# Transposing attention by DMA, as two planes of half words, in place of TensorE

## The chip, the cores, the metric

One core of a Trainium2 chip. The metric is the device time of the whole program in microseconds (us).

## The reference

Two graph layers over 128 batches of 128 tokens with 512 features. Layer 0 is attention with 8 heads of 64, whose scores are multiplied by twice the adjacency matrix before the softmax; layer 1 is a graph attention that the change does not touch.

```python
q, k, v = (proj(Wq, bq), proj(Wk, bk), proj(Wv, bv))
scores = jnp.einsum('bhqd,bhkd->bhqk', q, k) * SCALE
mask = (adj_matrix + bond_matrix)[:, None, :, :]
attn = jax.nn.softmax(scores * mask, axis=-1)
ctx = jnp.einsum('bhqk,bhkd->bhqd', attn, v)          # needs attn with k on the partitions
```

The scores come out with q on the partitions, and the context product wants k there, so each head's 128x128 block of attention, in fp32, has to be transposed.

## The kernel before

It works on pairs of batches, a and b, in one turn of a loop of 67. Products of the next group ("units", one call of `unit()`), the output product of the turn before (`output0`) and layer 1 of the turn before that (`output1`) are woven between the pieces of attention, so that TensorE has always something to do. Each engine runs its instructions in the order in which they are written here.

```python
def attn_T(b):
    at = ats[b][0]
    pa = ps2.tile([P, H, S], F32, name="pa", tag="ps2")
    for j in range(H):
        nc.tensor.transpose(pa[:, j, :], at[:, j, :], ident)   # TensorE, 8 heads
    aT = work.tile([P, H, S], F32, name="aT")
    nc.scalar.copy(aT, pa)                                     # ScalarE, PSUM to SBUF
...
# one turn, cut to a's and b's attention; o and e are the turns of output0 and output1
    scores(a); unit()()
    ...exps, normalise(a)...
    gather1(e, 0); gather1(e, 1); unit
    attn_T(a)
    output1(e, 0); output1(e, 1); unit
    context(a); unit()()
    scores(b)
    ...exps, normalise(b)...
    attn_T(b); hidden1(o); unit()(); output1(e, 5); output1(e, 6)
    context(b)
```

`context` ends with a ScalarE copy of its result to `cxT`; `unit()()` is a product and its eviction, in even turns often a ScalarE copy to v.

Of the kernel before, what the change touches and what calls it, by code (L numbers as in the profile page):

```python
# [7 lines left out]

F32 = mybir.dt.float32
AF = mybir.ActivationFunctionType  # L10
OP = mybir.AluOpType
AX = mybir.AxisListType

P = 128
# [3 lines left out]
H = 8  # L18
# [5 lines left out]
def kernel(  # L24
# [70 lines left out]
    def load_adjT(p):  # L95
        adjTs[p] = aio.tile([P, 2, S], F32, name="adjT")
        nc.sync.dma_start(adjTs[p], both(adjT, p))
# [71 lines left out]

        return mv, stats, power  # L170

    st0, rows0, qks, vs, ats, l1s, zs = {}, {}, {}, {}, {}, {}, {}

    def stats0(p, src):
        st0[p], stats, power = row_stats(src)
# [25 lines left out]

    def fetch0(p):
        r = rows0[p]
        rows0[p] = small.tile([P, 2, 2 * S], F32, name="mr", bufs=2)
        nc.sync.dma_start(
            rows0[p].rearrange("p s k -> p (s k)"), r.rearrange("s b p -> (s b p)").partition_broadcast(P)
        )
# [98 lines left out]
    def scores(b):  # L306
        p, i = divmod(b, 2)
        g, h = divmod(p, 2)
        qT, kT = qks[g, "q"][h], qks[g, "k"][h]
        cols = slice(i * S, (i + 1) * S)  # L310

        sc = ps2.tile([P, H, S], F32, name="sc", tag="ps2")
        for j in range(C):
            for s in range(2):
                r = slice(s * D, (s + 1) * D)
                nc.tensor.matmul(sc[:, s * C + j, :], qT[r, j, cols], kT[r, j, cols], start=True, stop=True)  # L316
        at = work.tile([P, H, S], F32, name="at")
        nc.vector.scalar_tensor_tensor(  # L318
            at, sc, QSCALE, adjs[p][:, i : i + 1, :].to_broadcast([P, H, S]), op0=OP.mult, op1=OP.mult
        )  # L320
        nmx = small.tile([P, H], F32, name="nmx")
        nc.vector.tensor_reduce(nmx, at, AX.X, OP.max, negate=True)  # L322
        ats[b] = at, nmx, small.tile([P, H], F32, name="sums")

    def exps(b, heads):
        at, nmx, sums = ats[b]
        for j in heads:
            nc.scalar.activation(at[:, j, :], at[:, j, :], AF.Exp, bias=nmx[:, j : j + 1], accum_out=sums[:, j : j + 1])  # L328

    def normalise(b):  # L330
        at, _, sums = ats[b]
        rs = small.tile([P, H], F32, name="rs")
        nc.vector.reciprocal(rs, sums)
        nc.vector.tensor_tensor(at, at, rs[:, :, None].to_broadcast([P, H, S]), OP.mult)  # L334

    def attn_T(b):
        at = ats[b][0]
        pa = ps2.tile([P, H, S], F32, name="pa", tag="ps2")
        for j in range(H):
            nc.tensor.transpose(pa[:, j, :], at[:, j, :], ident)  # L340
        aT = work.tile([P, H, S], F32, name="aT")
        nc.scalar.copy(aT, pa)  # L342
        ats[b] = aT


    cxT = const.tile([P, 7, 2, S], F32, name="cxT")
# [5 lines left out]
    def context(b):  # L352

        p, i = divmod(b, 2)
        aT = ats.pop(b)
        pc = ps1.tile([P, C, S], F32, name="pc", tag="ps1")
        for j in range(C):
            for s in range(2):
                head = 2 * j + s
                nc.tensor.matmul(  # L360
                    pc[s * D : (s + 1) * D, j, :], vs[b // G][:, b % G, head * D : (head + 1) * D], aT[:, s * C + j, :],
                    start=True, stop=True,
                )
        nc.scalar.copy(rows_of(cxT, i), pc)  # L364
# [74 lines left out]
    def scale1(p):  # L439
        h2, w, sums = l1s[p]  # L440
        rs = small.tile([P, 2], F32, name="rs1")
        nc.vector.reciprocal(rs, sums)
        nc.vector.tensor_tensor(w, w, rs[:, :, None].to_broadcast([P, 2, S]), OP.mult)  # L443
        l1s[p] = h2, w, work.tile([P, 7, 2, S], F32, name="gT")
# [97 lines left out]
    with tc.manual_schedule():  # L542
# [28 lines left out]
        for p in range(N + 3):  # L571
            g, odd = divmod(p, 2)
            units = (SEQ[10:] if odd else SEQ[:10]) if (g + 1) * 2 < N else []
            units = iter(units)

            def unit():
                u = next(units, None)
                return product(g + 1, u[0], int(u[1])) if u else lambda: None

            attn = p < N  # L580
            o = p - 1 if 0 <= p - 1 < N else None
            e = p - 2 if 0 <= p - 2 < N else None
            f = p - 3 if 0 <= p - 3 < N else None
            h = p + 4 if p + 4 < N else None
            a, b = 2 * p, 2 * p + 1


            if o is not None:
                load_adjT(o)
            if p + 1 < N:  # L590
                load_adj(p + 1)
            if h is not None:
                fetch0(h)
                load_xT(h)
            if p + 5 < N:
                load_x0(p + 5)
            if attn:
                scores(a)
            unit()()

            if e is not None:
                scores1(e)
            if attn:
                exps(a, range(4))
            if o is not None:

                first, second = output0(o, 0), output0(o, 1)
                first()
                second()
            if e is not None:  # L610
                softmax1(e)
            if p == 1:
                spread_u()
            done = unit()
            if e is not None:
                scale1(e)
            done()
            if attn:
                exps(a, range(4, H))

            if o is not None:
                output0(o, 2)()
            done = unit()
            if attn:
                normalise(a)
            done()
            if f is not None:
                finish_a(f)

            if e is not None:  # L630
                gather1(e, 0)
                gather1(e, 1)
            done = unit()
            if f is not None:
                finish_b(f)
            done()
            if e is not None:
                gather_sums(e)

            if attn:  # L640
                attn_T(a)
            if e is not None:
                first, second = output1(e, 0), output1(e, 1)
                first()
                second()
            if o is not None:
                context_sums(1)
            if attn and p > 2:
                load_x(p)
            done = unit()  # L650
            done()
            if h is not None:
                hidden(h)

            if attn:
                context(a)
            unit()()
            if p + 5 < N:
                stats0(p + 5, x0s.pop(p + 5))

            if attn:
                scores(b)
            if o is not None:
                output0(o, 3)()
            if p == 0:
                constant_c()
                weight_sums(wo_sb)
            unit()()
            if attn:
                exps(b, range(4))  # L670

            if o is not None:
                output0(o, 4)()
            if e is not None:
                output1(e, 2)()
            if attn:
                exps(b, range(4, H))
            unit()()
            if odd and (g + 2) * 2 < N:
                hidden_sums(g + 2)  # L680
            if p + 5 < N:
                spread0(p + 5)

            if o is not None:
                output0(o, 5)()
                stats1(o, 0)
            if attn:
                normalise(b)
            if e is not None:
                output1(e, 3)()  # L690
            unit()()

            if o is not None:
                output0(o, 6)()
                stats1(o, 1)
            if e is not None:
                output1(e, 4)()
            done = unit()
            if attn:
                shift(p)  # L700
            done()

            if attn:
                attn_T(b)
            if o is not None:
                hidden1(o)
            unit()()
            if e is not None:
                output1(e, 5)()
            if o is not None:  # L710
                dots1(o, 0)
            if e is not None:
                output1(e, 6)()
            if attn:
                context(b)
            if o is not None:
                dots1(o, 1)
            if e is not None:
                elu(e)
            if attn:  # L720
                context_sums(0)
            if p == 0:
                constant_u()
                weight_sums(w1_sb)
# [42 lines left out]
```

## Time and profile before

| | before |
|---|---|
| median of 4 runs | 2589.59 us (2589.25 to 2589.99) |
| TensorE, VectorE, ScalarE busy | 98%, 79%, 50% |
| mean granted clock of TensorE | 0.993 |
| one pair of turns, even and odd | 78.3 us |

Busy is the share of the span in which an engine worked; the granted clock is the share of full speed that TensorE was given. In the profiles below PE is TensorE, PEld its loading of weights, DVE VectorE, ACT ScalarE, POOL GpSimd and SPq the queue that issues DMAs; the chain is the work that ended last, followed back from the last instruction through what each step waited for. pa are the transposes, sc the scores, pc the contexts, acc the units' products, row the output products of both layers, gT the evicted gathers; sp and tp are the planes before and after the DMA; x16 counts instructions. The pair of turns was read as the time from one scores product to the fourth after it, which is the same for nearly all pairs. The lines are shown in the prediction.

### The profile page before, as it was taken

How to read it: one execution, taken by the hardware profiler on the slowest of the kernel's cores; microseconds unless marked ns; L12 is line 12 of the kernel's file. 1: busy time of each engine (PE TensorE's matmuls, PEld its weight loads, DVE VectorE, ACT ScalarE, POOL GpSimd, SP SyncE). 2: the span in 40 equal slices, each digit the busy share in tenths (PEclk: the TensorE clock that was granted, in tenths of full speed). 3: DMA queues.
4: the chain of work that ended last, by engine and by line, in shares of the span. 5: the costliest groups of instructions: out<-in, count | busy, mean ns of one | idle time of the engine just before them, and what ended most of it. 6: DMA issues, size and time to landing. Idle time of an engine off the chain costs nothing.

```text
span 2589.1 us, 40551 instructions
## 1 busy us (share of the span) xinstructions
PE 2531.6 (98%) x15288; PEld 2162.4 (84%) x15288; DVE 2050.1 (79%) x3781; ACT 1300.3 (50%) x3915; POOL 119.7 (5%) x263
## 2 busy tenths in 40 slices
PE   8899999999999999999999999999999999999986
PEld 7788888888888888888888888888888888888875
DVE  5677888878888878888878888878888878887775
ACT  3345455455554554554554554454554555555553
POOL 0000000000000000000000000000000000000000
PEclk9899999999999999999999999999999999999998
DMA  3122222222222222222222222222222222221001
GB/s 138 50 62 66 63 77 66 61 78 66 61 75 69 61 71 74 61 70 69 66 63 79 62 65 66 74 66 62 78 66 62 78 66 61 78 66 54 30 31 43
DMA packets 192868, 171.84 MB, mean 66 GB/s; under 512 B 41376, under 2 KB 135584, under 8 KB 192032
## 3 DMA queue, kind: packets, MB, share of 16 engines
q1 hardware_dynamic: 191088, 169.24, 22.8%
q8 instruction: 120, 1.97, 0.4%
q14 instruction: 76, 0.62, 0.2%
q10 hardware_dynamic: 1584, 0.01, 0.0%
HBM read 135.53 MB, written 33.68 MB: 65 GB/s over the span
## 4 chain that ended last, share of the span: by engine, by line
PE 80%; DVE 9%; ACT 7%; issue 3%; DMA 1%; POOL 0%; SPq 0%; POOLq 0%; DVEq 0%; ACTq 0%
PE acc_a L249 21%; PE row_a L301 16%; PE acc_c L249 11%; PE row_c L301 8%; PE acc_b L249 6%; PE pg L451 5%; PE pa L340 4%; PE sc L316 4%; DVE junk L413 4%; PE pc L360 4%; ACT at L328 2%; DVE at L318 2%; ACT aT L342 1%; ACT w L436 1%; ACT qT L266 1%
## 5 line engine op out<-in xcount | busy, mean ns | idle before, releaser
L328 ACT ACTIVATE at<-at,nmx 128x128 f32<-128x128 f32 x1024 | 396.4, 389 | 34.3 <-DVE nmx L322 32.0
L301 PE MATMUL row_a<-wo,cxT 128*128 128x256 f32 x1280 | 323.1, 383 | 10.9 <-DVE x L374 10.6
L301 PE MATMUL row_a<-w,gT 128*128 128x256 f32 x1280 | 319.0, 380 | 1.8 <-ACT z L478 0.9
L301 PEld LDWEIGHTS row_a<-wo,cxT 128*128 128x128 f32 x1280 | 236.0, 191 | 48.5 <-DVE x L374 20.4
L301 PEld LDWEIGHTS row_a<-w,gT 128*128 128x128 f32 x1280 | 235.9, 191 | 31.1 <-ACT z L478 1.7
L266 ACT ACTIVATE kT<-acc_a,bk 128x256 f32<-128x256 f32 x256 | 107.1, 470 | 290.9 <-PE acc_a L249 290.9
L328 ACT ACTIVATION_READ_ACCUMULATOR at<-at,nmx 128x1 f32 x1024 | 192.8, 188 | 0.0
L163 DVE BATCH_NORM_STATS2 st<-x 128x6 f32<-128x512 f32 x256 | 175.1, 684 | 8.9 <-DMA x<-in_x 4.5
L261 ACT COPY v<-acc_a 128x512 f32<-128x512 f32 x128 | 75.0, 586 | 185.3 <-PE acc_a L249 185.3
L342 ACT COPY aT<-pa 128x1024 f32<-128x1024 f32 x128 | 129.6, 1012 | 74.9 <-PE pa L340 70.1
L266 ACT ACTIVATE qT<-acc_a,bq 128x256 f32<-128x256 f32 x256 | 106.7, 467 | 110.9 <-PE acc_a L249 110.9
L334 DVE TENSOR_TENSOR at<-at,rs 128x1024 f32<-128x1024 f32 x128 | 156.8, 1225 | 4.4
L322 DVE TENSOR_REDUCE nmx<-at 128x8 f32<-128x1024 f32 x128 | 156.2, 1220 | 4.4
L374 DVE TENSOR_TENSOR x<-row_a,x 128x256 f32<-128x256 f32 x320 | 134.9, 422 | 31.2 <-PE row_a L301 24.7
L318 DVE SCALAR_TENSOR_TENSOR at<-sc,adj 128x1024 f32<-128x1024 f32 x128 | 154.3, 1206 | 4.5 <-PE sc L316 4.5
L316 PEld LDWEIGHTS sc<-kT,qT 64*128 64x128 f32 x2048 | 125.0, 188 | 32.2 <-issue 32.2
L451 PEld LDWEIGHTS pg<-w,h 128*128 128x128 f32 x1024 | 127.7, 200 | 26.7 <-ACT qT L266 15.2
L316 PE MATMUL sc<-kT,qT 64*128 64x128 f32 x2048 | 149.7, 286 | 0.0
L360 PEld LDWEIGHTS pc<-aT,v 128*64 128x64 f32 x2048 | 109.9, 137 | 43.6 <-issue 32.2
L364 ACT COPY cxT<-pc 128x512 f32<-128x512 f32 x128 | 75.0, 586 | 141.5 <-PE pc L360 136.6
L451 PE MATMUL pg<-w,h 128*128 128x128 f32 x1024 | 133.6, 286 | 12.1 <-DVE w L443 5.1
L360 PE MATMUL pc<-aT,v 128*64 128x128 f32 x2048 | 140.9, 280 | 1.1 <-ACT aT L342 1.1
(130 smaller groups left out, 5052.9 us busy)
## 6 DMA issues: line engine op xcount, KB each, us to landing
x<-in_x SPq DMA_DIRECT2D x123, 512.0 KB, 4.6
out<-x SPq DMA_DIRECT2D x64, 512.0 KB, 2.8
hA<-in_xT SPq DMA_DIRECT2D x120, 256.0 KB, 4.2
mr<-rows SPq DMA_DIRECT2D x60, 256.0 KB, 4.2
adj<-in_adj SPq DMA_DIRECT2D x64, 128.0 KB, 10.7
adjT<-in_adjT SPq DMA_DIRECT2D x64, 128.0 KB, 9.0
x<-in_x SPq DMA_DIRECT2D x4, 256.0 KB, 3.9
wv<-in_wvT SPq DMA_DIRECT2D x1, 1024.0 KB
```

The lines of the kernel that those rows point to most:

```text
L163: nc.vector.bn_stats(st, src[:, i, :])
L249: nc.tensor.matmul(acc[:, m, :], lhsT, rhs, start=fresh and m == 0 and c == 0, stop=c == 1, skip_group_check=True)
L266: nc.scalar.activation(dst(t, f)[:, m, :], a[:, m, :], AF.Identity, bias=bias[:, j : j + 1])
L301: nc.tensor.matmul(acc, left[:, la, c, :], w[:, wb, c, :], start=n in (0, 3) and c == 0, stop=c == 1, skip_group_check=True)
L316: nc.tensor.matmul(sc[:, s * C + j, :], qT[r, j, cols], kT[r, j, cols], start=True, stop=True)
L318: nc.vector.scalar_tensor_tensor(at, sc, QSCALE, adjs[p][:, i : i + 1, :].to_broadcast([P, H, S]), op0=OP.mult, op1=OP.mult)
L322: nc.vector.tensor_reduce(nmx, at, AX.X, OP.max, negate=True)
L328: nc.scalar.activation(at[:, j, :], at[:, j, :], AF.Exp, bias=nmx[:, j : j + 1], accum_out=sums[:, j : j + 1])
L334: nc.vector.tensor_tensor(at, at, rs[:, :, None].to_broadcast([P, H, S]), OP.mult)
L342: nc.scalar.copy(aT, pa)
L360: nc.tensor.matmul(pc[s * D : (s + 1) * D, j, :], vs[b // G][:, b % G, head * D : (head + 1) * D], aT[:, s * C + j, :], start=True, stop=True,
L451: nc.tensor.matmul(pg[:, c, :], h2[:, i, c * P : (c + 1) * P], w[:, i, :], start=True, stop=True)
```

## The change

The intent is to take the transposes, 8 matmuls a batch, from TensorE. The DMA engines can transpose elements of two bytes, so ScalarE parts each half of the normalised attention (4 heads) into two planes of half words, one DMA transposes both, and ScalarE joins them to words again. The contexts are moved: a's stands directly before b's scores, b's in the next turn before the next scores.

```diff
-    def attn_T(b):
...
+    def words(a):
+        return a.rearrange("p h k -> p (h k)").bitcast(U16).rearrange("p (k w) -> p w k", w=2)
+
+    def part(b, half):
         at = ats[b][0]
...
+        sp = work.tile([P, 2, C * S], U16, name="sp", bufs=2)
+        nc.scalar.copy(sp, words(at[:, half * C : (half + 1) * C]))
+        tp = work.tile([P, 2 * C, S], U16, name="tp", bufs=2)
+        nc.sync.dma_start_transpose(tp, sp.rearrange("p w k -> p (w k)"))
+        flips[b, half] = tp
+
+    def join(b, half):
...
+        tp = flips.pop((b, half))
+        nc.scalar.copy(words(aTs[b][:, half * C : (half + 1) * C]), tp.rearrange("p (w h) k -> p w (h k)", w=2))
...
+                context(2 * o + 1)          # start of a turn: b of the turn before, then scores(a)
...
-                normalise(a)
+                normalise(a, 1)
             done()
+            if attn:
+                part(a, 1)                  # part(a, 0) a little earlier
...
-                attn_T(a)
...
+            unit()()
+            if attn:
+                join(a, 0)
+                join(a, 1)
...
                 context(a)
+                scores(b)                   # was one unit later
...
                 output1(e, 5)()
+            if attn:
+                join(b, 0)
             if o is not None:
                 dots1(o, 0)
             if e is not None:
                 output1(e, 6)()
-            if attn:
-                context(b)
             if o is not None:
                 dots1(o, 1)
+            if attn:
+                join(b, 1)
```

(The exps are also split otherwise, the first context sums stand later, and some buffers change their number.)

More of the change, by code (lines that the diff above doesn't have):

```diff
@@ L9 @@
 F32 = mybir.dt.float32
+U16 = mybir.dt.uint16
 AF = mybir.ActivationFunctionType
@@ L170, in row_stats @@
         return mv, stats, power
-    st0, rows0, qks, vs, ats, l1s, zs = {}, {}, {}, {}, {}, {}, {}
+    st0, rows0, qks, vs, ats, aTs, flips, l1s, zs = {}, {}, {}, {}, {}, {}, {}, {}, {}
     def stats0(p, src):
@@ L203, in fetch0 @@
         r = rows0[p]
-        rows0[p] = small.tile([P, 2, 2 * S], F32, name="mr", bufs=2)
+        rows0[p] = small.tile([P, 2, 2 * S], F32, name="mr", bufs=1)
         nc.sync.dma_start(
@@ L316, in scores @@
                 nc.tensor.matmul(sc[:, s * C + j, :], qT[r, j, cols], kT[r, j, cols], start=True, stop=True)
-        at = work.tile([P, H, S], F32, name="at")
+        at = work.tile([P, H, S], F32, name="at", bufs=2)
         nc.vector.scalar_tensor_tensor(
@@ L328, in exps, with normalise @@
             nc.scalar.activation(at[:, j, :], at[:, j, :], AF.Exp, bias=nmx[:, j : j + 1], accum_out=sums[:, j : j + 1])
-    def normalise(b):
+    def normalise(b, half):
         at, _, sums = ats[b]
-        rs = small.tile([P, H], F32, name="rs")
-        nc.vector.reciprocal(rs, sums)
-        nc.vector.tensor_tensor(at, at, rs[:, :, None].to_broadcast([P, H, S]), OP.mult)
-    def attn_T(b):
-        at = ats[b][0]
-        pa = ps2.tile([P, H, S], F32, name="pa", tag="ps2")
-        for j in range(H):
-            nc.tensor.transpose(pa[:, j, :], at[:, j, :], ident)
-        aT = work.tile([P, H, S], F32, name="aT")
-        nc.scalar.copy(aT, pa)
-        ats[b] = aT
+        heads = slice(half * C, (half + 1) * C)
+        rs = small.tile([P, C], F32, name="rs")
+        nc.vector.reciprocal(rs, sums[:, heads])
+        nc.vector.tensor_tensor(at[:, heads], at[:, heads], rs[:, :, None].to_broadcast([P, C, S]), OP.mult)
+    def words(a):
+        return a.rearrange("p h k -> p (h k)").bitcast(U16).rearrange("p (k w) -> p w k", w=2)
+    def part(b, half):
+        at = ats[b][0]
+        sp = work.tile([P, 2, C * S], U16, name="sp", bufs=2)
[4 more added lines that the diff above has]
+    def join(b, half):
+        if half == 0:
+            aTs[b] = work.tile([P, H, S], F32, name="aT", tag="at", bufs=2)
+        tp = flips.pop((b, half))
+        nc.scalar.copy(words(aTs[b][:, half * C : (half + 1) * C]), tp.rearrange("p (w h) k -> p w (h k)", w=2))
     cxT = const.tile([P, 7, 2, S], F32, name="cxT")
@@ L354, in context @@
         p, i = divmod(b, 2)
-        aT = ats.pop(b)
+        aT = aTs.pop(b)
+        ats.pop(b)
         pc = ps1.tile([P, C, S], F32, name="pc", tag="ps1")
@@ L598 @@
                 scores(a)
+            if o is not None:
+                context_sums(0)
             unit()()
@@ L616 @@
                 scale1(e)
+            if attn:
+                exps(a, range(4, 6))
             done()
             if attn:
-                exps(a, range(4, H))
+                exps(a, range(6, H))
+                normalise(a, 0)
+                part(a, 0)
             if o is not None:
@@ L647 @@
                 context_sums(1)
+            unit()()
+            if attn:
+                join(a, 0)
+                join(a, 1)
             if attn and p > 2:
                 load_x(p)
-            done = unit()
-            done()
             if h is not None:
@@ L661 @@
             if attn:
-                scores(b)
+                exps(b, range(4))
             if o is not None:
@@ L669 @@
             if attn:
-                exps(b, range(4))
+                exps(b, range(4, H))
+                normalise(b, 0)
+                part(b, 0)
             if o is not None:
@@ L675 @@
                 output1(e, 2)()
+            done = unit()
             if attn:
-                exps(b, range(4, H))
-            unit()()
+                normalise(b, 1)
+            done()
+            if attn:
+                part(b, 1)
             if odd and (g + 2) * 2 < N:
@@ L686 @@
                 stats1(o, 0)
-            if attn:
-                normalise(b)
             if e is not None:
@@ L701 @@
             done()
-            if attn:
-                attn_T(b)
             if o is not None:
@@ L709 @@
                 output1(e, 5)()
+            if attn:
+                join(b, 0)
             if o is not None:
@@ L713 @@
                 output1(e, 6)()
-            if attn:
-                context(b)
             if o is not None:
                 dots1(o, 1)
+            if attn:
+                join(b, 1)
             if e is not None:
                 elu(e)
-            if attn:
-                context_sums(0)
             if p == 0:
```

## The prediction

> **What bounds the kernel now.** I read the page first, then the chain that ended last (twelve microseconds of it at two places), then ScalarE's timeline there, and busy time over one period. A period is one turn of the loop, two batches a and b; 64 turns of about 39.8 us make the run. Even turns compute v and some of q, odd turns the rest of q and k.
>
> ```profile
> span 2589.1 us, 40551 instructions
> PE 2531.6 (98%) x15288; PEld 2162.4 (84%) x15288; DVE 2050.1 (79%) x3781; ACT 1300.3 (50%) x3915; POOL 119.7 (5%) x263
> ...
> PE 80%; DVE 9%; ACT 7%; issue 3%; DMA 1%; POOL 0%; SPq 0%; POOLq 0%; DVEq 0%; ACTq 0%
> ...
> L342 ACT COPY aT<-pa 128x1024 f32<-128x1024 f32 x128 | 129.6, 1012 | 74.9 <-PE pa L340 70.1
> ...
> L364 ACT COPY cxT<-pc 128x512 f32<-128x512 f32 x128 | 75.0, 586 | 141.5 <-PE pc L360 136.6
> ```
>
> TensorE is the bound: it is busy 98% of the span and makes 80% of the chain, while ScalarE is busy 50%. Over one turn it has no idle time at all:
>
> ```profile
> 1228.10:1267.90 39.80, 39.80 (x254) 34.21 (x253) 30.77 (x59) 20.46 (x60) 1.85 (x4) 1.00 0.32 81
> ```
>
> The columns are length, then busy time of PE, PEld, DVE, ACT and POOL, granted clock, DMA share, GB/s. So what leaves TensorE is a gain, unless TensorE waits in its place. The two places where it would wait are the two contexts. The chain (start, length, what) around batch a's context of an even turn, with the transpose still in it:
>
> ```profile
> 1240.98 0.87 PE pa L340 x8
> 1241.85 1.73 PE row_a L301 x8
> 1243.58 1.73 PE acc_a L249 x8
> 1245.31 1.02 PE pc L360 x16
> 1246.33 1.92 PE acc_a L249 x8
> 1248.25 1.09 PE sc L316 x16
> ```
>
> and around batch b's context at the end of an odd turn:
>
> ```profile
> 1225.43 0.86 PE row_a L301 x4
> 1226.30 0.86 PE row_c L301 x4
> 1227.16 1.02 PE pc L360 x16
> 1228.18 1.09 PE sc L316 x16
> 1229.28 1.92 PE acc_a L249 x8
> ```
>
> ScalarE just before these contexts (two answers of its timeline):
>
> ```profile
> 1226.33 0.37 ACT L481 COPY z<-row_a 128x256 f32<-128x256 f32 x1
> ...
> 1245.34 0.59 ACT L261 COPY v<-acc_a 128x512 f32<-128x512 f32 x1 [1.35 <-PE acc_a L249]
> ```
>
> Each of these two copies starts 0.03 us after the product that it evicts is done, and TensorE has 0.86 us of work left before the context in the first case and none in the second. Now no matter, since aT is made long before. After the change the joins stand behind them in ScalarE's order.
>
> **What the Trainium skill says.** "ScalarE: Activation LUTs", section "What ACT_TABLE_LOAD costs": one element per cycle and lane, fp32 and bf16 alike, 186 ns plus 0.833 ns an element, back-to-back ones overlapping by about 93 ns. The trace agrees nearly: 1024 elements took 1012 ns (the formula gives 1039). Two-byte elements should thus bring no gain: a part or a join moves 1024 of them. "VectorE: DVE Perf Modes", section "The three transpose paths": a 128x128 bf16 transpose takes 1309 ns by DMA. "DMA: Bandwidth & Descriptors", section "Latency and other measured facts": 261 GB/s for a large DMA transpose. No run here has one yet. For the 256 KB of one transfer these give estimates of 1.0 us (bandwidth) to 10.5 us (eight blocks in turn), and the nearest in this trace, the 512 KB store, lands in 2.8 us. I take 3 to 4 us from issue to landing.
>
> **The change part by part.** All per pair of turns (79.6 us, four batches), since even and odd differ.
> - Removed from TensorE: four groups of eight transposes, 4 x 0.87 = 3.5 us. Contexts now always stand beside scores. In the chain a context or scores alone makes the product after it slower (1.92 for 1.73, 1.06 for 0.86), and one such step a turn goes: 2 x 0.2 = 0.4 us. Gain 3.9 us.
> - ScalarE: four aT copies (4.0 us) go; eight parts and eight joins come, 16 x about 0.95 us (1.0 less the overlap) = 15.2 us. About 41 us become 52 of 80: no bound on average.
> - VectorE: normalising by halves adds a reciprocal (0.17) and one overhead for each batch, some 1.2 us a pair; 31 of 40 us a turn stays below the bound.
> - DMA: 256 transposes of 256 KB, 67 MB beside 172 MB; the share of 0.2 to 0.4 has room. The sync queue is in order: transposes of b now stand ahead of the rows store, the broadcast and the loads that follow. The broadcast is issued about 9 us after the store, and lands in 4; its user comes some 15 us later in the turn than that. Slack enough.
> - Waits at the contexts, where the matter is decided:
>  - Even turn, a: the v product ends, v copy 0.5, two joins 0.9 + 1.0, context: TensorE idles 2.5 us, however early the transposes landed. Before the joins the transposes have time: the exps end about 9.3 us after the scores began, the parts about 11.8, the joins begin at 16.8, so 5 us for the last transfer.
>  - Odd turn, a: the product before the context is evicted by VectorE. From the weights of layer 1 (some 4.9 us after the scores) ScalarE has 0.6 + 3.1 (exps) + 0.8 + three pairs of q and k evictions 2.2 + parts 1.9 + gathers 1.1 + 0.3 + joins 1.9 = 11.9, ends at 16.8; TensorE would be there at 16.2. With a transfer of 3 to 4 us after the second part (12.6), 0.6 to 1.5: I take 0.9 us.
>  - Odd turn, b: z copy 0.3 and joins 1.9 behind row_a, less row_c's 0.86: 1.4 us.
>  - Even turn, b: there is no unit of products before the last two pieces, so the two activations of h are in the way: nmr was ready at 1262.9, h can run 1263.6 to 1265.1 without the aT copy, z to 1265.3, joins to 1267.2; TensorE, freed of pa, would want the context at 1264.4: 2.8 us.
>  Sum 2.5 + 0.9 + 1.4 + 2.8 = 7.6 us.
> - Net +3.7 us per pair, times 32: +118 us, 2707. Stalls partly overlap waits elsewhere, and the ends of the run have no products; I put 2690.
>
> **Rivals.**
> 1. The gain comes through: 128 x 0.87 = 111 us and 64 x 0.2 = 13 go, 2465 us. For it: TensorE's 98% against 50% of ScalarE, and a half period for the transfer. Against: the transfer may be hidden, yet the joins are not; they are queued right in front of the context, behind an eviction that TensorE has just released. Only joins at about half the duration would rescue it (net near zero, about 2585).
> 2. The DMA transpose is slow, towards 10 us, or holds the sync queue: the a contexts then wait 4 or 5 us more, 2 x 4.5 x 32 = 290 us, some 2980. For it: the page's 1309 ns for one block[...]. Against: its own figure for bandwidth, sixteen engines at a share of 0.2 to 0.4, and b's seven microseconds of slack.
> 3. ScalarE as bound: 26 us of a turn of 40. Only its order hurts, not its total.
>
> **Range and chances.** If all four stalls are as small as their hard parts (2.3, 0, 1.2, 1.5: 5 us), the sum is 2589 + 32 x 1.1 = 2625; a little below that is my low end. With 3 us more per pair from later transfers it is 2800, the high end. The 2% lines are 2538 and 2641. Slower is the likeliest at 0.70; within 2% 0.18; faster 0.12, for a mistake in the order of the engines or a cheaper join. Predicted 2690 us, 2605 to 2800.
>
> **What would show each step.** Right: TensorE busy near 2405 us (less transposes and steps), its idle time before pc some 3.8 us a turn on average and put down to ScalarE's aT copies; pc waiting 2 to 3 us in even turns and about 1 us in odd ones; part and join copies of 1.0 us each; transposes landing in 3 to 5 us. Wrong: no waits before pc; or joins that idle on the DMA for long (rival 2); or joins under 0.6 us. If scores, not contexts, wait, the chain is not the one that I worked out.

## The result, and the profile after

The changed kernel took 2941.07 us (median of 4, 2938.07 to 2943.22): slower, at 1.1356 of before (95% interval 1.1337 to 1.1376).

The page of the changed kernel, the lines that answer to those of before:

```profile
span 2936.3 us, 39562 instructions
PE 2573.5 (88%) x14264; PEld 2170.2 (74%) x14264; DVE 2099.6 (72%) x4037; ACT 1707.2 (58%) x4299; POOL 139.0 (5%) x263
...
PE 56%; ACT 27%; DVE 12%; issue 3%; DMA 2%; POOL 0%; SPq 0%; ACTq 0%; POOLq 0%; DVEq 0%
...
L373 PE MATMUL pc<-aT,v 128*64 128x128 f32 x2048 | 233.0, 326 | 273.0 <-ACT aT L355 273.0
...
L355 ACT COPY aT<-tp 128x1024 uint16<-128x1024 uint16 x256 | 324.7, 1334 | 15.4 <-DMA tp<-sp 15.4
...
L346 ACT COPY sp<-at 128x1024 uint16<-128x1024 uint16 x256 | 267.0, 1043 | 46.2 <-DVE at L336 43.6
...
tp<-sp SPq DMA_TRANSPOSE x256, 3.2
```

In a group's line the numbers after the first bar are busy time and the mean of one in ns, and after the second bar the idle time before them and what ended it. Four things are to be seen. TensorE idled 273.0 us in front of the contexts, released by the join (`aT<-tp`). ScalarE now makes 27% of the chain. The transposes landed in 3.2 us, and the joins waited for them only 15.4 us in all. And TensorE is busy 2573.5 us, more than before (2531.6), though 1024 matmuls are gone.

The last is answered by one pair of turns. The chain around batch a's context of an even turn, and then b's at its end:

```profile
2114.52 1.74 PE acc_a L250 x8
...
2116.29 0.03 ACT v L262
...
2116.77 2.53 ACT aT L355 x2
...
2119.34 1.97 PE pc L373 x14
2121.31 2.01 PE sc L317 x16
2123.32 3.11 PE acc_a L250 x8
...
2139.61 0.84 ACT qT L267 x2
2140.45 1.40 ACT h L419 x2
2141.85 0.26 ACT z L494
2142.11 2.43 ACT aT L355 x2
...
2144.59 1.09 PE pc L373 x14
```

The product ends, the v copy runs, two joins of 1.3 us run, then the context: this is the order that the prediction described, with longer joins. What it did not describe is the context itself, 1.97 us where it was 1.02, and the scores and the product after it, 2.01 for 1.09 and 3.11 for 1.92. Busy time by microseconds in this place (columns as in the prediction; the third from the end is the granted clock):

```profile
2118.00:2119.00 1.00, 0.43 (x2) 0.19 (x2) 0.97 (x2) 1.00 (x2) 0.00 (x0) 0.94 0.51 47
2119.00:2120.00 1.00, 0.66 (x6) 0.66 (x8) 0.98 (x1) 0.29 (x1) 0.00 (x0) 0.50 0.98 383
...
2125.00:2126.00 1.00, 1.00 (x4) 0.79 (x4) 1.00 (x2) 0.00 (x0) 0.00 (x0) 0.65 0.00 0
```

TensorE has been idle but for two matmuls since 2116.3; the clock falls to one half near 2119, and stays there until about 2125.7 although TensorE is full again. Three pieces that take 4.1 us at full clock took 7.1: 3.0 us lost, counted as busy.

TensorE's timeline gives the idle time before each context of this pair of turns (in brackets):

```profile
2118.15 0.43 PE L373 MATMUL pc<-aT,v 128*64 128x128 f32 x2 [1.90 <-ACT aT L355]
2119.34 1.97 PE L373 MATMUL pc<-aT,v 128*64 128x128 f32 x14 [0.76 <-ACT aT L355]
...
2143.39 0.43 PE L373 MATMUL pc<-aT,v 128*64 128x128 f32 x2 [2.09 <-ACT aT L355]
2144.59 1.09 PE L373 MATMUL pc<-aT,v 128*64 128x128 f32 x14 [0.76 <-ACT aT L355]
...
2159.82 1.99 PE L302 MATMUL row_a<-w,gT 128*128 128x256 f32 x8 [1.35 <-ACT gT L465]
2164.71 1.09 PE L373 MATMUL pc<-aT,v 128*64 128x128 f32 x14 [0.76 <-ACT aT L355]
...
2186.05 0.43 PE L373 MATMUL pc<-aT,v 128*64 128x128 f32 x2 [0.83 <-ACT aT L355]
2187.24 1.09 PE L373 MATMUL pc<-aT,v 128*64 128x128 f32 x14 [0.76 <-ACT aT L355]
```

So 2.66 (even, a), 2.85 (even, b), 2.11 (odd, a, of which 1.35 is layer 1's product waiting for the evictions of the gathers) and 1.59 us (odd, b), 9.2 us together. The first two matmuls of a context run after the first join and the rest after the second, so the second join is paid for on its own. The split has a price besides the idle time: the two pieces are busy 0.43 and 1.09 us, where the context took 1.02 us in one piece before, so 0.5 us more, 2.0 us for the four. With the clock's 3.0 us and less the 3.5 us of removed transposes this makes 10.7 us; a pair of turns grew by 10.4 (78.3 to 88.7; the pairs of the changed kernel range from 87.1 to 91.3). 31 such pairs are 322 of the 347 us between the two spans.

A gap does not always cost clock. In this pair b's gap (2.09 and 0.76 us) left it at 1.00; 600 us earlier the same gap lowered it, and the context's second piece took 1.97 us:

```profile
1520.46 0.43 PE L373 MATMUL pc<-aT,v 128*64 128x128 f32 x2 [2.09 <-ACT aT L355]
1521.64 1.97 PE L373 MATMUL pc<-aT,v 128*64 128x128 f32 x14 [0.75 <-ACT aT L355]
```

Over the whole run the second piece was slow (over 1.2 us) in 28 of the 32 contexts of even a, 14 of even b, 1 of odd a and 2 of odd b. The trace's clock record gives a reason: all 55 starts of low clock lie on one grid of 3.413 us, and 53 of the 55 stretches last one or two steps of it. So where a gap falls on this grid seems to matter, and not only how long it is; no run moved a gap on purpose to test it.

### The profile page after: what moved, and what is told of

The parts are those of the page before. It is cut to its first block, busy times and chain, and to the rows that moved or that the text cites. A ratio compares the mean times of both kernels' runs of the same rounds, so it can differ in the third digit from the quotient of the medians.

```text
span 2936.3 us, 39562 instructions
## 1 busy us (share of the span) xinstructions
PE 2573.5 (88%) x14264; PEld 2170.2 (74%) x14264; DVE 2099.6 (72%) x4037; ACT 1707.2 (58%) x4299; POOL 139.0 (5%) x263
## 4 chain that ended last, share of the span: by engine, by line
PE 56%; ACT 27%; DVE 12%; issue 3%; DMA 2%; POOL 0%; SPq 0%; ACTq 0%; POOLq 0%; DVEq 0%
PE acc_a L250 14%; PE row_a L302 12%; ACT aT L355 10%; PE acc_c L250 8%; PE sc L317 6%; PE pc L373 6%; PE row_c L302 6%; ACT at L329 4%; ACT sp L346 3%; DVE at L319 3%; DVE nmx L323 3%; PE acc_b L250 2%; ACT qT L267 2%; ACT w L449 2%; ACT h L419 2%
## 5 line engine op out<-in xcount | busy, mean ns | idle before, releaser
L373 PE MATMUL pc<-aT,v 128*64 128x128 f32 x2048 | 233.0, 326 | 273.0 <-ACT aT L355 273.0
L373 PEld LDWEIGHTS pc<-aT,v 128*64 128x64 f32 x2048 | 163.5, 161 | 355.2 <-ACT aT L355 355.2
L302 PE MATMUL row_a<-w,gT 128*128 128x256 f32 x1280 | 326.4, 386 | 47.4 <-ACT gT L465 44.5
L355 ACT COPY aT<-tp 128x1024 uint16<-128x1024 uint16 x256 | 324.7, 1334 | 15.4 <-DMA tp<-sp 15.4
L346 ACT COPY sp<-at 128x1024 uint16<-128x1024 uint16 x256 | 267.0, 1043 | 46.2 <-DVE at L336 43.6
L317 PE MATMUL sc<-kT,qT 64*128 64x128 f32 x2048 | 187.2, 335 | 0.0
L336 DVE TENSOR_TENSOR at<-at,rs 128x512 f32<-128x512 f32 x256 | 177.2, 692 | 8.8
L317 PEld LDWEIGHTS sc<-kT,qT 64*128 64x128 f32 x2048 | 159.9, 235 | 29.1 <-issue 29.1
L168 POOL TENSOR_SCALAR mv<-mv 128x2 f32<-128x2 f32 x128 | 41.6, 325 | 2759.3 <-DVE mv L165 1754.2
L440 ACT ACTIVATE w<-w,ws 128x128 f32<-128x128 f32 x128 | 44.4, 394 | 176.9 <-DVE w L438 176.9
```

The costliest lines, as they stand in the source:

```text
L302: nc.tensor.matmul(acc, left[:, la, c, :], w[:, wb, c, :], start=n in (0, 3) and c == 0, stop=c == 1, skip_group_check=True)
L317: nc.tensor.matmul(sc[:, s * C + j, :], qT[r, j, cols], kT[r, j, cols], start=True, stop=True)
L336: nc.vector.tensor_tensor(at[:, heads], at[:, heads], rs[:, :, None].to_broadcast([P, C, S]), OP.mult)
L346: nc.scalar.copy(sp, words(at[:, half * C : (half + 1) * C]))
L355: nc.scalar.copy(words(aTs[b][:, half * C : (half + 1) * C]), tp.rearrange("p (w h) k -> p w (h k)", w=2))
L373: nc.tensor.matmul(pc[s * D : (s + 1) * D, j, :], vs[b // G][:, b % G, head * D : (head + 1) * D], aT[:, s * C + j, :], start=True, stop=True,
```

## The experiments

Theory: the loss is the joins standing in ScalarE's order directly in front of the context, behind an eviction that TensorE has just released, and the granted clock after the idle time. Rivals: the work of parts and joins as such, the DMA, the new order of the pieces, or the form of the joins. All results are correct. The first four runs shared one chip, and so did the last three; each was timed in 3 rounds against the kernel before, whose median was 2589.59 us beside the changed kernel, 2590.92 and 2589.32 us in these two groups. So medians of different groups can be compared here.

| run | median us | ratio to before (95%) |
|---|---|---|
| changed kernel | 2941.07 | 1.1356 (1.1337 to 1.1376) |
| e_joinb, b's joins early | 2765.06 | 1.0681 (1.0652 to 1.0711) |
| e_pe, new order with TensorE's transposes | 2600.64 | 1.0038 (1.0023 to 1.0052) |
| e_warm, products that keep TensorE busy | 2848.97 | 1.1004 (1.0988 to 1.1021) |
| e_dense, joins that write densely | 2868.84 | 1.1077 (1.106 to 1.1093) |
| e_alate, a's context late | 2784.18 | 1.0745 (1.0727 to 1.0763) |
| e_best1, together | 2523.52 | 0.9752 (0.9731 to 0.9772) |
| e_best2, together, both parts late | 2514.48 | 0.9709 (0.9695 to 0.9724) |

**e_joinb.** The same instructions, two of them earlier in ScalarE's order.

```diff
+            if attn:
+                join(b, 0)
+                join(b, 1)
             if e is not None:
                 output1(e, 4)()
...
-            if attn:
-                join(b, 0)
...
-            if attn:
-                join(b, 1)
```

> The two joins of batch b moved up in ScalarE's order, to where it idles some 4.5 us after b's parts; the work is the same. Theory (place in the order): TensorE's idle time before b's contexts, 2.85 us in an even and 1.59 us in an odd turn of the changed kernel, goes; 4.4 us x 32 = 142 us, so about 2800 us, and joins of 1.3 us as before. Rival 1 (the work of ScalarE as such): unchanged within 1%, about 2940. Rival 2 (slow transposes): the joins now idle 2 us or more on the DMA, and little is gained.

Measured: 2765 us, 176 less. The waits of this run, total and number:

```profile
PE pc L373 <- ACT aT L355: 130.1, 99, 12.7
```

against 273.0 us in 226 waits in the changed kernel: 143 us less, as worked out (142), with joins of 1.34 us as before. The remaining 33 us are more than the idle time; part of it is clock, whose mean rose from 0.953 to 0.969. So the place in the order cost 6%, with the same work and the same DMAs. One sign of rival 2 did come: the joins now waited for transposes 46 times, 109.2 us in all (15.4 in the changed kernel). But its consequence, that little is gained, did not: ScalarE had that time to spare.

**e_pe.** The order of the changed kernel, with `attn_T` at its old place and the copy behind it.

```diff
-                part(a, 0)                  # and the three others, and the four joins
+            if attn:
+                attn_T(a)                   # before output1(e, 0); attn_T(b) after hidden1(o)
```

> The changed order kept (contexts beside scores, normalising by halves, exps split), but the transposes on TensorE and one ScalarE copy as in the kernel before. Theory (the loss is all parts and joins): 2575 to 2600 us, the kernel before less a little for the saved switch between contexts and scores. Rival (the new order itself costs): over 2650 us.

Measured: 2600.64 us, 0.4% above before and just above the expected range; the saving of 0.4 us a pair that I had put on contexts beside scores is not seen (a pair takes 78.5 us, before 78.3). The new order neither costs nor gains anything that matters. The loss is in parts, transposes, joins and what follows from them.

**e_warm.**

```diff
         pc = ps1.tile([P, C, S], F32, name="pc", tag="ps1")
+        if (p % 2 == 0):
+            for _ in range(6):
+                nc.tensor.matmul(pc[:, 0:2, :], wv_sb[:, 0, 0, 0:P], wv_sb[:, 0, 0, :], start=True, stop=True, skip_group_check=True)
```

> Six products of 128x256 that nothing reads are put in front of the contexts of even turns, so that TensorE is busy there while it waits. Theory (idle time costs a second time, in the granted clock): the clock of 0.5 after the even context goes, pc and sc take 1.1 us each and the next product 1.9, 3 us a pair of turns less, some 2850 to 2880 us. Rival (the slow contexts come from their own form or from something else): 2941 us or more.

Measured: 2848.97 us, 92 less, by adding 384 products that nobody reads. The groups of the scores in this run and in the changed kernel:

```profile
L317 PE MATMUL sc<-kT,qT 64*128 64x128 f32 x2048 | 153.7, 291 | 0.0
```

```profile
L317 PE MATMUL sc<-kT,qT 64*128 64x128 f32 x2048 | 187.2, 335 | 0.0
```

The mean granted clock is 0.989 (changed kernel 0.953), and in the 90 us from 2000 on it is 1.00 on average, with every context piece at 1.09 us. So 92 us of the loss was the clock after idle time, close to the 3.0 x 32 = 96 that the one pair had given.

**e_dense.** The joins walk the words of aT in order and take half words from the two planes in turn.

```diff
-        nc.scalar.copy(words(aTs[b][:, half * C : (half + 1) * C]), tp.rearrange("p (w h) k -> p w (h k)", w=2))
+        nc.scalar.copy(
+            words(aTs[b][:, half * C : (half + 1) * C]).rearrange("p w k -> p k w"),
+            tp.rearrange("p (w h) k -> p (h k) w", w=2),
+        )
```

> The joins write the words of aT densely and read the two planes in turn, in place of writing every second half word; same result. Theory (what makes a join 1.33 us where a part takes 1.04 is the scattered two-byte write): joins of about 1.05 us, 8 x 0.28 = 2.2 us a pair off the path, about 2870 us or somewhat less. Rival (a join is long for another reason): 1.33 us and 2941 us.

Measured: 2868.84 us, 72 less, and this from the joins' view:

```profile
L355 ACT COPY aT<-tp x256: 1146/1165/1179, 75.7 to 2818.7; 128x1024 uint16<-128x1024 uint16 x128
```

(shortest, median, longest in ns). The join fell from 1332 to 1165 ns, not to the 1045 of a part. Which elements are written one after another does set its duration; what the last 120 ns are is open. The time fell as expected although the join shortened less: the waits at the contexts are 34 us shorter (238.9 for 273.0), layer 1's for the gathers 9 us (35.6 for 44.5), and the clock helped too (mean 0.963 for 0.953).

**e_alate.**

```diff
             if attn:
-                context(a)
                 scores(b)
             unit()()
+            if attn:
+                context(a)
```

> Batch a's context moved behind the next scores and one more unit of products, so that TensorE has some 3 us of work while ScalarE joins; b as in the changed kernel. Theory (the waits come from the joins standing directly in front of the context): in an even turn the 2.66 us of idle time and the 3.0 us of low clock after it go, in an odd one 0.8 us: 160 to 205 us less, 2735 to 2780. Rival (the chain from a's scores to its context is too long as a whole, so the wait only moves to the context's new place): under 60 us less.

Measured: 2784.18 us, 157 less, just outside the expected range. Its waits:

```profile
PE pc L373 <- ACT aT L355: 158.1, 135, 9.2
...
PE row_c L302 <- ACT cxT L377: 20.2, 30, 0.7
```

115 us of waiting for a's joins are gone, and 20 us are new: directly behind a late context TensorE's next piece, in even turns, waits for the copy of that context. This is one part of the shortfall; the clock is another. Its mean rose only to 0.965, where e_warm had 0.989, because it now falls more often after b's wait: the second piece of even b's context was slow in 23 of 32 turns, in the changed kernel in 14. The wait did not move to the new place, so the chain from a's scores to its context is not too long as a whole.

**e_best1 and e_best2.** All of e_joinb, e_dense and e_alate; the first context sums behind `scores1`; and a's second part (e_best1) or both of a's parts (e_best2) behind the evictions of the gathers:

```diff
                 gather1(e, 0)
                 gather1(e, 1)
+            if attn:
+                part(a, 0)
+                part(a, 1)
```

> All together: b's joins early, a's context late, dense joins, a's second part behind the evictions of the gathers, the first context sums behind the scores of layer 1. Theory: the effects add, 142 + 180 + 70 less what they share (the clock), so 2550 to 2640 us; a chain from h over VectorE's dots to the next scores' mask, seen in the run with the early joins, keeps it from the 2465 us that the freed matmuls alone would give. Rival (ScalarE's total work binds): above 2700 us.

> As the run with all together, but both of a's parts behind the evictions of the gathers. Theory (the first part delays the gathers, on which layer 1's products wait 1.35 us in odd turns): 10 to 40 us less than with one part behind them. Rival (the later transposes then make the joins wait on the DMA): the same or longer.

Measured: 2523.52 us and 2514.48 us, the first 26 us below the expected range, the second 9 us better than the first where 10 to 40 were expected: both expectations were missed. The second had counted on layer 1's wait of 1.35 us for the gathers, but in e_best1 only 7.6 us of it were left in the whole run (44.5 in the changed kernel). e_best2 is 2.9% faster than the kernel before. Its page and waits:

```profile
PE 2421.7 (96%) x14264; PEld 2066.7 (82%) x14264; DVE 2068.7 (82%) x4037; ACT 1676.0 (67%) x4299; POOL 147.1 (6%) x263
...
PE 84%; ACT 6%; DVE 4%; DMA 4%; issue 1%; SPq 0%; POOL 0%; POOLq 0%; ACTq 0%; DVEq 0%
```

```profile
PE pc L376 <- ACT aT L355: 25.0, 11, 10.6
PE row_c L302 <- ACT cxT L380: 20.5, 30, 0.7
```

TensorE makes 84% of the chain again. The 273 us before the contexts are 25, in eleven places. The joins do now wait for transposes (150 us in all), mostly while TensorE has other work: its own waits at the contexts are the 25 us. DMA's share of the chain is 4%, so whether these waits still cost something is not settled. Nearly all pairs of turns take 75.0 to 76.3 us, against 78.3, so 2.0 to 3.3 us less, of the 3.5 us of the removed transposes; the wait for the context's copy is part of what is missing. The whole is 75 us, not 111.

## Why the prediction was wrong

It forecast slower, for the reason that held, but 2690 us (2605 to 2800) and not 2941.

The net of a pair of turns was predicted as +3.7 us and measured as +10.4. Of the difference of 6.7, the clock makes 3.0, the split contexts 2.0, longer waits 1.6 and a smaller gain 0.4 (7.0 by these estimates from one pair).

- **Waits at the contexts**, predicted for even a, even b, odd a, odd b as 2.5, 2.8, 0.9 and 1.4 us (7.6): measured 2.66, 2.85, 2.11 and 1.59 (9.2). The mechanism is shown by e_joinb and e_alate: the same joins elsewhere in ScalarE's order take the waits away.
- **The step that failed most** is the one that added the waits as if TensorE resumed at full speed. Waits at the contexts were counted once; many of the long ones, most of even a's, also lowered the granted clock, 3.0 us a pair in the pair shown, and 92 us of the run as e_warm shows. A page of the Trainium skill that the prediction does not name warns of it (last section). Nor did it count that a context that starts after the first join is split: 2.0 us a pair.
- **"16 x about 0.95 us (1.0 less the overlap)"** for parts and joins: the part was nearly right (1.04 us), the join took 1.33. I took two-byte elements to cost what others do and did not think of how they are written. Eight joins of 0.28 us more are 2.2 us a pair; a shorter join, 0.17 us less, was worth 72 us (e_dense). Some of the waits above contain this term.
- **Odd turn, a** took no account of who waits for the gathers: the two parts stood in front of their evictions, and layer 1's product waited 1.35 us. With the second part behind them 7.6 us of such waits are left in the run (e_best1), with both parts none is listed (e_best2). The 12.6 us for the end of the second part does not follow from the terms before it, which give 13.5; the trace has 13.1 (2158.80 less 2145.67).
- **The gain** of 3.9 us: 3.5 for the transposes is borne out by TensorE's busy time in e_best2 (2421.7 for 2531.6 us, 110 less); the 0.4 for contexts beside scores is not (e_pe).
- **Rival 2** was rightly put aside: transposes landed in 3.2 us and joins waited 15.4 us for them. The 261 GB/s that the estimate took for a "large" transpose stand in "DMA: Bandwidth & Descriptors", section "Latency and other measured facts", without a size and for a non-contiguous middle dimension. **Rival 1** was right in one sense: the gain is there, if the joins are out of the way. I had written that only joins of half the duration would rescue it; changing their place does.
- The numbers that I named as signs were "TensorE busy near 2405 us" (2573.5, for the clock) and "its idle time before pc some 3.8 us a turn" (273 / 64 = 4.3).
- **The period** was misread: the window 1228.10:1267.90 reaches into the next turn, whose scores started at 1266.31. A pair of turns is 78.3 us, not 79.6. Gains and waits do not rest on it.

## What to carry to other kernels

When work moves from a full engine to one with time to spare, look at where the new instructions stand in that engine's order, not at its share: an instruction that the full engine needs must not be queued behind one that this engine has only just released. Put the producer where its engine idles, and the consumer behind at least as much other work as the producer takes. And do not count an idle gap of some 3 us on TensorE once only: after it the clock can fall, as it did in 28 of even a's 32 contexts here and in 2 of odd b's 32, whose gaps are shorter, and this can cost as much again.

## What the Trainium skill lacked or had wrong

- "TensorE: Matmul & The Clock Gate", section "Why this matters for your kernels", asks for no idle gaps above about 3 us; Part 1 says that the clock falls after at least one idle window of some 3.4 us, and that the window is free-running. The traces agree with the window: the 55 starts of low clock in the changed kernel lie on one grid of 3.413 us. But TensorE need not be idle in it: in the window 2115.46:2118.88 it was busy 1.22 us, and the clock fell to 0.50 for the next two windows, 6.8 us; before the fall at 1521.54 it had been 0.67 us. The windows 2139.36:2142.77 and 2142.77:2146.18, over which b's gap was spread, had 1.94 and 2.03 us of work, and no fall came. The page does not say how much work in a window keeps the clock up.
- "ScalarE: Activation LUTs", section "What ACT_TABLE_LOAD costs", gives one element a cycle for fp32 and bf16 alike. A copy of 1024 half words took 1045 ns (median) when it read every second half word, 1332 when it wrote every second one, and 1165 when it wrote in order and read two planes in turn. The page has nothing on how strides change it; "SBUF — State Buffer" speaks of strides, but has no times for a ScalarE copy.
- "VectorE: DVE Perf Modes", section "The three transpose paths", has 1309 ns for one 128x128 block by DMA. Eight such blocks in one transfer, from SBUF to SBUF, landed in 3.2 us from the issue, of which the queue was held 1.26 us. No page has a measured time by which a transfer of this size holds the queue that issues it.
